# A tuned attention + low-rank FFN kernel: one more matrix product made "joint" over two pairs, its result added by GpSimd, and the memory copy centred after its transpose

## Chip, cores and metric

One core of a Trainium2 chip. The metric is the time on the device, in microseconds (us), of one launch of the whole program; lower is better. The kernel before is at 1116.14 us (median of three runs, 1115.12 to 1116.19).

## What is computed

```python
# x (8, 1024, 1024); ctx (8, 64, 1024); mask (8, 64); all float32
# attention to a small memory, per batch
scores = layernorm(x) @ ctx^T / sqrt(1024), masked to -1e30
x = x + softmax(scores) @ ctx            # zero where no row of the memory is valid
# feed-forward: a dense product and two of eight low-rank experts
h = layernorm(x)
base = h @ W^T                           # 1024 x 1024
w = top-2 of softmax(h @ router^T), normed to sum 1     # 8 experts
x = x + base + 2 * sum_e w_e * (h @ A_e^T) @ B_e^T      # rank 16
```

## The kernel before

**Tiles and pairs.** x has 64 tiles of 128 rows. Two tiles make a pair (32 pairs), four pairs are one batch and share one memory. Pairs 0 and 1 are done in `first()`, the others two at a time in 15 calls of `quad(u)` (u = 2, 4, ..., 30). A quad works on the FFN of pairs u and v = u+1, and beside it on the attention of the pairs that follow: n = u+2, m = u+3, f = u+4. In every other quad (u = 4, 8, ..., 24) f begins a new batch, so that a new memory is set up (`new_mem`).

**Order.** `manual_schedule` keeps the order in which the program text issues instructions. Each engine's queue works in that order and waits at its head. The order is thus written by hand: between products, or in `hooks` that a product calls after one of its blocks of matmuls, stand the small steps of the other pairs. An operation that waits holds up all that stands behind it on its engine.

**The dense product.** Each pair holds the transposed h in two tiles, hA (first half of the 1024 inputs) and hB (second half). With the two tiles as rows, base is a 2 x 2 block product, done in Strassen's form with 7 products in place of 8: GpSimd makes sums of the h blocks (`block_sums`, L566; s1 to s4), the sums of the weights t1 to t4 are made once. Products 1 to 7 of 512 columns are added to x by VectorE where they belong; "product 8" is the low-rank part alone (`lora`, L638). PE writes them into banks of PSUM, of which there are six for this.

**Joint products.** Products 7, 3, 5, 2, 4 of pairs u and v are taken together (`joint`, L720): u above v is a 2 x 2 product again, in halves of 256, and goes by the same form a second time: seven blocks of four matmuls of 256 columns, in place of two products of eight matmuls of 512 columns. The sums of the operands are made by GpSimd too (`joint_sums`, L701), the sums of the weights once (`quarter_sums`, L621). In a joint, `to_x` (L741) adds each part to x from PSUM; products 5 and 7 belong to two places of x (`BOTH`, L686), so each part is added twice.

Product 1 and product 6 are not joint. They run one after the other into one bank "ch" of each pair (`product`, L654): product 1 is added to x at (0,0); then product 6 is accumulated on top, and the bank is added at (0,1) and (1,0) (`chain_add`, L679); then product 8, added at (1,1). (The indices are tile of rows, half of columns.)

**Steps beside them.** `att_turn` (L367) transposes the raw x of a pair for the scores, on VectorE; `att_scores` (L371) is sct on PE and its copy scts on ScalarE; `att_sc` (L389) transposes the scores back on PE; `att_exp` and `att_divide` (L394, L411) are the softmax; `att_turn_p` (L418) transposes it, `att_readout` (L424) multiplies by the memory, `att_add` adds four banks to x. `f_sums`, `f_squares`, `f_std`, `f_rows` (L238 to L276) normalise on ScalarE and send h to DRAM; it comes back in blocks of 32 and `rt_turn_tile` (L502) transposes it. `rt_low_rank_tile` (L518) is the low-rank and router product, `rt_top` (L529) the top-2 weights on VectorE, `rt_turn_low_rank` (L558; trw on PE) turns the weighted result for `lora`.

**The memory.** `load_mem` (L111) loads a batch's ctx twice, for rows 0 to 63 and 64 to 127. A second form, centred (its mean taken off, so that the scores need no mean of x) and transposed, is made over four steps: `mem_stats` (mean), `send_mem` (L320, centred on ScalarE, to DRAM), `fetch_mem` (L332, back in blocks of 32), `turn_mem` (L338, transposed on VectorE). `void_mem` scales the uncentred one by the batch's validity.

Of the kernel before, what the change touches and what calls it, by code (L numbers as in the profile page):

```python
# [24 lines left out]
def kernel(  # L25
# [85 lines left out]
    def load_mem(b: int, halves=(0, 1)):  # L111
        if b not in mems:
            mems[b] = memp.tile([2 * M, D], F32, tag="mem", name=f"mem_{b}")
        for h in halves:
            nc.sync.dma_start(out=mems[b][h * M : (h + 1) * M, :], in_=mem[b])
# [147 lines left out]

    def f_rows(u: int, fetch: bool = True):

        nm, std, of_f = fts.pop(u)
        rstd, nmr = of_f[:, 4], of_f[:, 5]
        nc.vector.reciprocal(rstd, std)
        tt(nmr, nm, rstd, ALU.mult)  # L269
        for r in range(2):  # L270
            h = ring.tile([P, D], F32, tag="ring", name=f"h_{u}_{r}")
            hss.setdefault(u, []).append(h)
            nc.scalar.activation(  # L273
                h, xts[u][r], AF.Identity, bias=nmr[:, r, :], scale=rstd[:, r, :]
            )
        norm_send(u, fetch)  # L276
# [43 lines left out]
    def send_mem(b: int, by_vector: bool = False):  # L320

        if by_vector:
            mc = centre_mem(b, False)
        else:
            mv = mcs[b, "mv"]
            nc.scalar.mul(mv[:M, 1:2], mv[:M, 0:1], -1.0)
            mc = ring.tile([P, D], F32, tag="ring", name=f"memc_{b}_False")
            nc.scalar.activation(mc[:M], mems[b][:M], AF.Identity, bias=mv[:M, 1:2])
        mcs[b] = dram.tile([M, D], F32, tag="md", name=f"md_{b}", bufs=2)
        nc.sync.dma_start(out=mcs[b], in_=mc[:M])  # L330

    def fetch_mem(b: int):  # L332
        msr = ring.tile([P, D], F32, tag="ring", name=f"ms_{b}")
        ms = msr[:, : M // NB * QD].rearrange("p (t c) -> p t c", c=QD)
        load_blocked(ms, mcs[b])
        mcs[b, "ms"] = ms

    def turn_mem(b: int):  # L338
        mt = memp.tile([P, KD, M], F32, tag="memT", name=f"memT_{b}_True", bufs=1)
        transpose_blocked(mt, mcs[b, "ms"])  # L340
        mem_ts[b, True] = mt

# [150 lines left out]
    def h_tiles(u: int):  # L493
        has[u] = turned.tile([P, 2, KH, P], F32, tag="hA", name=f"hA_{u}")
        hbs[u] = turned.tile([P, 2, KH, P], F32, tag="hB", name=f"hB_{u}", bufs=3)

    def rt_turn_pe(u: int, r: int):
        if r == 0:
            h_tiles(u)
        transpose_pe((has[u][:, r], hbs[u][:, r]), hss[u][r], f"h{u}_{r}")  # L500

    def rt_turn_tile(u: int, r: int):  # L502
        if r == 0:
            h_tiles(u)
        half = KH * NB
        for t, c in ((has[u], 0), (hbs[u], half)):
            transpose_blocked(t[:, r], hss[u][r][:, :, c : c + half])
# [10 lines left out]
    def rt_low_rank_tile(u: int, r: int):  # L518
# [3 lines left out]
        for k in range(KD):  # L522
            h = (has[u] if k < KH else hbs[u])[:, r, k % KH, :]
# [42 lines left out]
    def block_sums(outs, a11, a12, a21, a22):  # L566

        s1, s2, s3, s4 = outs

        by = nc.gpsimd.tensor_tensor  # L570

        def one():
            by(s1, a21, a22, ALU.add)  # L573
            by(s2, s1, a11, ALU.subtract)

        def two():
            by(s4, a12, s2, ALU.subtract)  # L577
            by(s3, a11, a21, ALU.subtract)

        return one, two  # L580


    places = ["qa", "qb", "qc", "qd"]

    def in_place(i: int, name: str):
        return sums.tile([P, 2, HK, P], F32, tag=places[i], name=name)

    def rt_sums_steps(u: int, to=(0, 1)):

        sms[u] = sums.tile([P, 2, KH, P], F32, tag="s14", name=f"s14_{u}", bufs=2)  # L590
        s2, s3 = [
            in_place(i, f"s{j}_{u}").rearrange("p h k i -> p (h k) i")
            for i, j in zip(to, (2, 3))
        ]
        outs = sss[u] = sms[u][:, 0], s2, s3, sms[u][:, 1]
        ha, hb = has[u], hbs[u]
        return block_sums(outs, ha[:, 0], hb[:, 0], ha[:, 1], hb[:, 1])
# [3 lines left out]
    def rt_sums(u: int, to=(0, 1)):  # L601
        for do in rt_sums_steps(u, to):
            do()
# [17 lines left out]
    def quarter_sums(name: str, w):  # L621
# [5 lines left out]
        by(q3, b22, b12, ALU.subtract)  # L627
        by(q2, q3, b11, ALU.add)
        by(b12, b12, b11, ALU.subtract)
        by(q4, b21, q2, ALU.subtract)  # L630
        quarters[name] = b11, b21, b22, b12, q2, q3, q4

# [21 lines left out]
    def product(u: int, i: int, between=None, after: int = 0):  # L654
# [8 lines left out]
        elif i == 6:  # L663
            block(chain, sss[u][1], t2, False, between, after)
        elif i == 7:
            block(chain, sss[u][2], t3, False, between, after)
# [12 lines left out]
    def chain_add(u: int):  # L679

        for to in ((0, 1), (1, 0)):
            add(u, pps[u][1], *to)

# [4 lines left out]
    def joint_plain(i: int, p: int, between=None, after: int = 0):  # L688
# [4 lines left out]
            2: (hbs[p][:, 0], w21), 3: (sms[p][:, 1], w22), 4: (hbs[p][:, 1], t4)  # L693
# [4 lines left out]

    jss = {}

    def joint_sums(i: int, u: int):  # L701

        if i == 7:
            s12 = in_place(0, f"s12_j7_{u}")
            s43 = in_place(2, f"s43_j7_{u}")
            outs = jss[7] = s12[:, 0], s12[:, 1], s43[:, 1], s43[:, 0]
            up, lo = [sss[p][2] for p in (u, u + 1)]
            return block_sums(outs, up[:, :HK], up[:, HK:], lo[:, :HK], lo[:, HK:])
        outs = [
            in_place(k, f"s{j}_j{i}_{u}") for k, j in zip((3, 1, 2, 0), (1, 2, 3, 4))  # L710
        ]
        of_pair = sms if i == 5 else hbs
        up, lo = of_pair[u], of_pair[u + 1]
        for r, j in ((0, 5), (1, 3)) if i == 5 else ((0, 2), (1, 4)):
            jss[j] = [o[:, r] for o in outs]
        return block_sums(
            outs, up[:, :, :HK], up[:, :, HK:], lo[:, :, :HK], lo[:, :, HK:]
        )

    def joint(i: int, u: int, hooks, final: bool = False):  # L720
# [4 lines left out]

        v = u + 1
        r, c = L2.get(i, (None, None))
        a, d = [
            {
                2: lambda: hbs[p][:, 0], 3: lambda: sms[p][:, 1], 4: lambda: hbs[p][:, 1],  # L730
                5: lambda: sms[p][:, 0], 7: lambda: sss[p][2],
            }[i]()
            for p in (u, v)
        ]
        s1, s2, s3, s4 = jss.pop(i)
        name = {2: "w21", 3: "w22", 4: "t4", 5: "t1", 7: "t3"}[i]
# [4 lines left out]
        def to_x(p, src, first: int, n: int):  # L741
            for row, col in BOTH.get(i, ((r, c),)):
# [79 lines left out]
    def first():  # L822
# [47 lines left out]
        def plain(r: int, c: int, k: int, between=None):  # L870

            if k == 0:
                banks[r, c] = bank_of(f"plain_{r}_{c}")
            block(
                banks[r, c], (has, hbs)[k][0][:, r], blk[k + 1, c + 1], k == 0, between
# [17 lines left out]
        load_mem(1)  # L893
# [39 lines left out]
        rt_sums(1, (2, 3))  # L933
# [6 lines left out]
        weight_sums((t1, w12, w11, ALU.subtract))  # L940
# [19 lines left out]
        send_mem(1, True)  # L960
        fetch_mem(1)
# [3 lines left out]
        att_readout(3)  # L965
        x_stats(4)
# [5 lines left out]
        void_mem(1)  # L972
# [3 lines left out]
        quarter_sums("t1", t1)  # L976
        product(1, 7)
        quarter_sums("t3", t3)
        product_add(1, 7)
        turn_mem(1)  # L980
# [4 lines left out]
        quarter_sums("w22", w22)  # L985
        product_add(1, 8)
        rt_turn(2)
# [7 lines left out]
        quarter_sums("w21", w21)  # L995
        att_scores(4)

        def last():
            end()
            store(1, 1)  # L1000
            att_rstd(4)
# [6 lines left out]
    def quad(u: int):  # L1008
# [8 lines left out]
        if more and u > 2:  # L1017
            att_turn(m)
            x_sums(m)
        pending.pop()()  # L1020
        product_add(u, 1)
        if u == 2:
            att_divide(n)
        rt_low_rank_tile(u, 0)
        rt_low_rank_tile(u, 1)
        product(u, 6, (lambda: att_turn_p(n)) if u == 2 else None, 1)
        if u == 2:
            att_turn(m)
        if more:
            rt_top(u)  # L1030
            rt_turn(v)
        else:
            rt_turn_tile(v, 0)
            rt_top(u)
            rt_turn_tile(v, 1)
        if more and u > 2:
            x_squares(m)
            x_root(m)
        if new_mem:
            fetch_mem(b)  # L1040
        chain_add(u)
# [3 lines left out]
        if more:  # L1045
            att_readout(n)
            att_scores(m)
            rt_turn_low_rank(u)
            att_add(n)

        low_u = {1: lambda: rt_turn_low_rank(u)}
        if more:
            low_u = {0: lambda: att_sc(m)}
        low_u[2] = lambda: product(u, 8)
        one, two = rt_sums_steps(v, (2, 3))
        one()
        two()
        product(v, 1, low_u)
        if more:
            att_rstd(m)  # L1060
            att_exp(m)
        product_add(u, 8)
        product_add(v, 1)
        one, two = joint_sums(7, u)
        one()
# [3 lines left out]
        if new_mem:  # L1069
            mask_bias(b)  # L1070
            turn_mem(b)
        rt_low_rank_tile(v, 0)
        rt_low_rank_tile(v, 1)
        product(v, 6, (lambda: att_turn_p(m)) if more else None, 1)
        two()
# [5 lines left out]
        chain_add(v)  # L1081
        if more:
            f_std(n)
            f_rows(n)
            att_readout(m)
        if far:
            att_scores(f)
        if more:
            rt_turn_low_rank(v)
            att_add(m)  # L1090
        def low_v():
# [3 lines left out]
        if more:  # L1095
            hooks = {4: [low_v]}
        else:
            hooks = {1: [lambda: rt_turn_low_rank(v)], 3: [low_v]}
        if new_mem:
            void_mem(b)  # L1100
        if (f + 2) % PPB == 0 and f + 2 < NP:
            load_mem((f + 2) // PPB)
            load_mask((f + 2) // PPB)
        if far:
            x_stats(f)
            hooks[3] = [lambda: att_sc(f)]
        end_7 = joint(7, u, hooks)
        one, two = joint_sums(5, u)
        one()
        two()  # L1110

        hooks = {1: [end_7]}
# [3 lines left out]
        if more:  # L1116
            f_sums(m)
# [104 lines left out]
```

## Time and profile before

| | |
|---|---|
| time, median of three runs | 1116.14 us (1115.12 to 1116.19) |
| the profiled execution: time / span | 1115.52 / 1113.7 us |
| granted TensorE clock | 1.00 |
| one quad, from product 1 of u to the next | 67.64 us |
| busy in a quad (443.22 to 510.86): PE, PEld | 67.56, 50.29 us |
| DVE, ACT, POOL | 47.78, 38.17, 23.09 us |

The span is what the profiler recorded of one execution. PE is TensorE's matmuls, PEld its weight loads, DVE is VectorE, ACT ScalarE, POOL GpSimd, SP the queue that issues the DMAs. "L647 ch<-t,s" names the line of the code and the tiles: the output ch from operands t and s. A number behind x counts instructions. In brackets stands the idle time ahead of an instruction and who ended it. A row's duration of a matmul group includes the time in which the last one drains; the difference of two starts tells what a group costs in the queue.

### The profile page before, as it was taken

How to read it: one execution, taken by the hardware profiler on the slowest of the kernel's cores; microseconds unless marked ns; L12 is line 12 of the kernel's file. 1: busy time of each engine (PE TensorE's matmuls, PEld its weight loads, DVE VectorE, ACT ScalarE, POOL GpSimd, SP SyncE). 2: the span in 40 equal slices, each digit the busy share in tenths (PEclk: the TensorE clock that was granted, in tenths of full speed). 3: DMA queues.
4: the chain of work that ended last, by engine and by line, in shares of the span. 5: the costliest groups of instructions: out<-in, count | busy, mean ns of one | idle time of the engine just before them, and what ended most of it. 6: DMA issues, size and time to landing. Idle time of an engine off the chain costs nothing.

```text
span 1113.7 us, 16669 instructions
## 1 busy us (share of the span) xinstructions
PE 1104.8 (99%) x5670; PEld 805.6 (72%) x5670; DVE 771.4 (69%) x2009; ACT 589.2 (53%) x1083; POOL 383.7 (34%) x344
## 2 busy tenths in 40 slices
PE   8999999999999999999999999999999999999998
PEld 6555686776867778687786867768677786877867
DVE  6685777757777676776767767686776767766564
ACT  4577455827458373673827548274583736635010
POOL 0048353234333243233333332343332432333341
PEclk9999999999999999999999999999999999999999
DMA  9956366273653646446373553745446463442401
GB/s 228 228 186 202 116 179 208 76 246 121 182 171 118 210 146 179 144 154 213 107 224 125 160 191 96 246 139 165 150 137 208 149 188 115 154 149 77 151 1 76
DMA packets 105477, 175.80 MB, mean 158 GB/s; under 512 B 13040, under 2 KB 77552, under 8 KB 105392
## 3 DMA queue, kind: packets, MB, share of 16 engines
q1 hardware_dynamic: 105392, 174.73, 50.5%
q8 instruction: 45, 0.74, 0.3%
q14 instruction: 40, 0.33, 0.1%
HBM read 107.84 MB, written 66.85 MB: 157 GB/s over the span
## 4 chain that ended last, share of the span: by engine, by line
PE 98%; DMA 1%; SPq 0%; issue 0%; ACT 0%; DVE 0%; DVEq 0%; ACTq 0%
PE jl L647 24%; PE ch L647 19%; PE ju L647 18%; PE pa L524 11%; PE ro L431 6%; PE sct L377 5%; PE ju L639 3%; PE jl L639 3%; PE plain L647 3%; PE ch L639 2%; PE trw L562 1%; PE j L647 1%; DMA w<-in_w_t_dram 1%; PE b L647 0%; PE plain L639 0%; PE ptp L420 0%
## 5 line engine op out<-in xcount | busy, mean ns | idle before, releaser
L744 DVE TENSOR_TENSOR xt<-jl,xt 128x256 f32<-128x256 f32 (+1 forms) x421 | 191.9, 486 | 130.2 <-PE jl L647 111.7
L744 DVE TENSOR_TENSOR xt<-ju,xt 128x256 f32<-128x256 f32 (+1 forms) x210 | 110.8, 552 | 61.7 <-PE ju L647 60.8
L573 POOL TENSOR_TENSOR s<-hA,hB 128x512 f32<-128x512 f32 x31 | 39.6, 1278 | 306.7 <-DVE hB L89 251.1
L195 ACT ACTIVATE junk<-xt 128x1024 uint8<-128x1024 f32 x60 | 63.3, 1056 | 127.6 <-DMA xt<-in_x_dram 127.1
L647 PE MATMUL ch<-t,s 128*128 128x512 f32 x256 | 116.9, 592 | 0.0
L647 PE MATMUL ch<-w,hA 128*128 128x512 f32 x248 | 115.9, 593 | 0.0
L636 DVE TENSOR_TENSOR xt<-ch,xt 128x512 f32<-128x512 f32 x124 | 82.1, 681 | 20.4 <-PE ch L639 13.1
L647 PE MATMUL jl<-t,s_j 128*128 128x256 f32 x360 | 93.4, 382 | 1.1
L647 PE MATMUL ju<-w,s_j 128*128 128x256 f32 x360 | 94.0, 383 | 0.0
L273 ACT ACTIVATE h<-xt,of_f 128x1024 f32<-128x1024 f32 x60 | 71.3, 1234 | 21.3 <-DVE of_f L269 20.7
L647 PEld LDWEIGHTS jl<-t,s_j 128*128 128x128 f32 x360 | 65.9, 190 | 22.2 <-issue 12.7
L636 DVE TENSOR_TENSOR xt<-ro,xt 128x512 f32<-128x512 f32 x128 | 79.6, 679 | 3.4 <-PE ro L431 3.4
L647 PEld LDWEIGHTS ju<-w,s_j 128*128 128x128 f32 x360 | 64.2, 190 | 16.6 <-DVE xt L744 5.8
L647 PEld LDWEIGHTS ch<-t,s 128*128 128x128 f32 x256 | 45.0, 190 | 42.9 <-issue 42.9
L647 PEld LDWEIGHTS ch<-w,hA 128*128 128x128 f32 x248 | 44.7, 190 | 43.0 <-issue 42.0
L89 DVE STREAM_TRANSPOSE xT<-xs 128x1024 f32<-128x1024 f32 x60 | 72.5, 1228 | 2.7 <-DMA md<-memc_False 1.8
L524 PEld LDWEIGHTS pa<-art_sb,hA 128*128 128x128 f32 x512 | 66.3, 190 | 9.0 <-issue 4.7
L577 POOL TENSOR_TENSOR s_j<-s,s_j 128x256 f32<-128x256 f32 (+1 forms) x30 | 30.1, 1002 | 117.8 <-PE ch L647 96.4
L524 PE MATMUL pa<-art_sb,hA 128*128 128x136 f32 x512 | 69.9, 279 | 0.0
L524 PE MATMUL pa<-art_sb,hB 128*128 128x136 f32 x512 | 69.7, 279 | 0.0
L204 ACT ACTIVATE junk<-xt,of_x 128x1024 uint8<-128x1024 f32 x60 | 68.7, 1145 | 1.5
L253 ACT ACTIVATE junk<-xt,of_f 128x1024 uint8<-128x1024 f32 x60 | 68.5, 1142 | 1.1
(179 smaller groups left out, 2206.4 us busy)
## 6 DMA issues: line engine op xcount, KB each, us to landing
xt<-in_x_dram SPq DMA_DIRECT2D x64, 512.0 KB, 4.6
out_dram<-xt SPq DMA_DIRECT2D x62, 512.0 KB, 3.5
xs<-in_x_dram SPq DMA_DIRECT2D x240, 128.0 KB, 3.6
hd<-h SPq DMA_DIRECT2D x60, 512.0 KB, 2.7
hs<-hd SPq DMA_DIRECT2D x240, 128.0 KB, 3.1
mem<-in_ctx_dram SPq DMA_DIRECT2D x16, 256.0 KB, 4.6
w<-in_w_t_dram SPq DMA_DIRECT2D x16, 256.0 KB, 10.3
md<-memc_False SPq DMA_DIRECT2D x7, 256.0 KB, 3.1
```

The lines of the kernel that those rows point to most:

```text
L89: nc.vector.transpose(dst.rearrange("p k (t i) -> p t k i", i=NB), src.rearrange("p t (k i) -> p t k i", i=NB),)
L195: nc.scalar.activation(nowhere, xts[u][r], AF.Identity, accum_out=sm[:, r, :])
L204: nc.scalar.activation(nowhere, xts[u][r], AF.Square, bias=nm[:, r, :], accum_out=ss[:, r, :],)
L253: nc.scalar.activation(nowhere, xts[u][r], AF.Square, bias=nm[:, r, :], accum_out=ss[:, r, :])
L273: nc.scalar.activation(h, xts[u][r], AF.Identity, bias=nmr[:, r, :], scale=rstd[:, r, :])
L377: mm(sct[r * M : (r + 1) * M, :], mt[:, k, :], x_ts[u][r][:, k, :], start=(k == 0), stop=(k == KD - 1),)
L431: mm(ro, pts[u][rows, :], m[rows, ts(c, HB)], start=True, stop=True)
L524: mm(pa[:, r, :], h, art_sb[:, k, :], start=(k == 0), stop=(k == KD - 1))
L636: tt(xc, bank, xc, ALU.add)
L639: mm(bank, axwts[u][:, r, :], lb_sb[:, c0 : c0 + n], start=alone, stop=True, skip_group_check=True)
L647: mm(bank, a[:, k, :], w[:, k, :], start=(start and k == 0), stop=(k == n - 1), skip_group_check=True)
L744: tt(xc, src, xc, ALU.add)
```

## The change

**Product 6 becomes joint**, as the first: the joints now go 6, 2, 7, 3, 5, 4. Its result isn't added to x by VectorE part by part, but put into a place of its own, t: the first half of hA, whose content is no longer needed by then (`t_of`). One 256-column part is copied by ScalarE, the other three by VectorE, and two of 512 columns are then added to t by VectorE. Then GpSimd adds t to x at three places for each of the two pairs (`six_add`, six adds of 128 x 512). Product 1 is added at (0,0), (0,1) and (1,0) by VectorE (`one_add`).

**Sums in place.** The third sum of a pair (`rt_sum_3`) overwrites hA's second half, that of a joint the half of the lower operand; joint sums are made for one product at a time. hB becomes a tile for each tile of rows.

**One memory copy.** The centred memory isn't sent to DRAM. `load_ms` loads ctx in blocks of 32 directly, `turn_mem` transposes it on VectorE and sums it over its eight chunks, `centre_turned` multiplies by ones of 1/1024 on PE (the mean of each row, in all partitions), and VectorE subtracts. The uncentred memory has one buffer, loaded after the last readout of the old one.

**Moved steps.** `att_turn_p` stands between the two low-rank tiles; `rt_turn_low_rank(u)` right after `att_scores(m)`; `rt_turn_low_rank(v)` in joint 6; `att_turn(m+2)` in joint 4 of the quad before; `f_rows(n)` in two steps in joint 6. In `first()`, GpSimd makes t1 and the sums of t2's quarters.

```diff
+    def load_ms(b: int):
+        msr = ring.tile([P, D], F32, tag="ring", name=f"ms_{b}")
+        n = M // NB * QD
+        ms = msr[:, :n].rearrange("p (t c) -> p t c", c=QD)
+        load_blocked(ms, mem[b])
+        ones = msr[:, n : n + P]
+        nc.gpsimd.memset(ones, 1.0 / D)
+        mcs[b] = ms, ones, msr[:, n + P : n + P + M]
     def turn_mem(b: int):
         mt = memp.tile([P, KD, M], F32, tag="memT", name=f"memT_{b}_True", bufs=1)
-        transpose_blocked(mt, mcs[b, "ms"])
+        ms, ones, of_k = mcs[b]
+        transpose_blocked(mt, ms)
+        nc.vector.tensor_reduce(of_k, mt.rearrange("p k m -> p m k"), AX.X, ALU.add)
         mem_ts[b, True] = mt
+    def centre_turned(b: int):
+        ms, ones, of_k = mcs.pop(b)
+        mt = mem_ts[b, True]
+        means = bank_of(f"means_{b}")[:, :M]
+        mm(means, ones, of_k, start=True, stop=True)
+        tt(mt, mt, means.unsqueeze(1).to_broadcast([P, KD, M]), ALU.subtract)
...
+    def one_add(u: int):
+        for to in ((0, 0), (0, 1), (1, 0)):
             add(u, pps[u][1], *to)
+    def t_of(u: int):
+        return has[u][:, 0].rearrange("p k i -> p (k i)")
+    def six_add(u: int):
+        for r, c in ((1, 0), (1, 1), (0, 1)):
+            xc = xts[u][r][:, ts(c, HB)]
+            nc.gpsimd.tensor_tensor(xc, xc, t_of(u), ALU.add)
...
         def to_x(p, src, first: int, n: int):
+            if i == 6:
+                t = t_of(p)[:, first : first + n]
+                if n == HH and p == u and first == 0:
+                    nc.scalar.copy(t, src)
+                elif n == HH:
+                    nc.vector.tensor_copy(t, src)
+                else:
+                    tt(t, src, t, ALU.add)
+                return
...
         product(u, 1, (lambda: att_sc(n)) if u == 2 else None, 1)
         if more and u > 2:
-            att_turn(m)
             x_sums(m)
+        if new_mem:
+            mask_bias(b)
         pending.pop()()
-        product_add(u, 1)
...
+        one_add(u)
         rt_low_rank_tile(u, 0)
...
         rt_low_rank_tile(u, 1)
-        product(u, 6, (lambda: att_turn_p(n)) if u == 2 else None, 1)
...
+        rt_turn_tile(v, 0)
+        rt_top(u)
+        rt_turn_tile(v, 1)
+        rt_sum_3(u)
+        rt_sums(v)
...
         if new_mem:
-            fetch_mem(b)
-        chain_add(u)
+            load_ms(b)
...
             att_readout(n)
             att_scores(m)
-            rt_turn_low_rank(u)
+            if u > 2:
+                rt_turn_low_rank(u)
+                x_root(m)
             att_add(n)
...
         product(v, 1, low_u)
...
             f_sums(n)
             att_divide(m)
         if new_mem:
-            mask_bias(b)
             turn_mem(b)
+        one_add(v)
         rt_low_rank_tile(v, 0)
+        if more:
+            att_turn_p(m)
+        if new_mem:
+            centre_turned(b)
         rt_low_rank_tile(v, 1)
-        product(v, 6, (lambda: att_turn_p(m)) if more else None, 1)
-        two()
+        joint_sums(6, u)
+        rt_sum_3(v)
         if far:
             att_turn(f)
         rt_top(v)
...
             att_readout(m)
         if far:
             att_scores(f)
+        if new_mem:
+            load_mem(b)
         if more:
-            rt_turn_low_rank(v)
             att_add(m)
+        hooks = {5: [lambda: rt_turn_low_rank(v)]}
...
+        end_6 = joint(6, u, hooks)
+        joint_sums(2, u)
+        def six():
+            end_6()
+            low_v()
+            for p in (u, v):
+                six_add(p)
+        hooks = {1: [six]}
...
-        end_7 = joint(7, u, hooks)
+        end_2 = joint(2, u, hooks)
+        joint_sums(7, u)
...
+        if m + 2 < NP:
+            hooks[5] = [lambda: att_turn(m + 2)]
         end_4 = joint(4, u, hooks, not more)
```

## The prediction

> **What bounds the kernel now.** I read the page's engine line and its chain of waits first, then PE's waits, then three equal stretches, then the timeline of one stretch.
>
> ```profile
> PE 1104.8 (99%) x5670; PEld 805.6 (72%) x5670; DVE 771.4 (69%) x2009; ACT 589.2 (53%) x1083; POOL 383.7 (34%) x344
> PE 98%; DMA 1%; SPq 0%; issue 0%; ACT 0%; DVE 0%; DVEq 0%; ACTq 0%
> ```
>
> PE is busy for 99% of the span, and the chain that ended last is PE for 98% of it. Any time is gained or lost on PE's queue: fewer matmuls, or a wait that PE doesn't have today. It has almost none: PE's longest waits are 1.6 us at the start and this one.
>
> ```profile
> PE ptp L420 <- DVE s L415: 1.0, 1, 1.0
> ```
>
> The stretches run from one product 1 of an even pair to the next, so each is one quad.
>
> ```profile
> 375.58:443.22 67.64, 67.56 (x353) 50.29 (x352) 48.02 (x125) 38.47 (x70) 23.11 (x21) 1.00 0.53 161
> 443.22:510.86 67.64, 67.56 (x353) 50.29 (x352) 47.78 (x126) 38.17 (x69) 23.09 (x21) 1.00 0.52 167
> 510.86:578.50 67.64, 67.56 (x353) 50.29 (x352) 48.01 (x125) 38.48 (x70) 23.10 (x21) 1.00 0.52 161
> ```
>
> The columns are PE, PEld, DVE, ACT, POOL, granted clock. The period is 67.64 us whether or not a new memory is set up (the middle one does it), at full clock. DVE has 20 us free, POOL 44 us. Fifteen such quads are the program; pairs 0 and 1 come before.
>
> **The matmuls.** One full product is 8 matmuls of 512 columns, and a joint one has seven blocks of 4 matmuls of 256 columns in place of two products.
>
> ```profile
> 450.80 3.60 PE L647 MATMUL ch<-t,s 128*128 128x512 f32 x8
> 454.33 1.99 PE L431 MATMUL ro<-mem,pt 64*128 64x512 f32 x8
> 456.25 1.97 PE L377 MATMUL sct<-xT,memT_True 128*64 128x128 f32 x32
> 458.15 0.44 PE L562 MATMUL trw<-ident,axl 128*128 128x128 f32 x2
> ```
>
> The first row is product 6. From its start to the next is 3.53 us, of which 0.09 is a gap that stands before ro anyway: 3.44. A block of a joint starts every 0.865 us (422.58, 423.44, 424.31 in the same timeline). Product 6 costs 2 x 3.44 = 6.88 us per quad now and 7 x 0.865 = 6.06 after: -0.82 us per quad, 15 quads, **-12.4 us**. Joints 5 and 7 lose 0.25 us each to waiting for two 256-column adds; joint 6 has one copy there, so I count none (to +0.25 a quad, 3.7 in all).
>
> **POOL.** Per quad it had 23.1 us. It gets: 8 adds of 512 columns for the sums of a pair (1.27 each), 24 of 256 for six joints (0.73), 6 of 512 that add t to x (1.27): 10.2 + 17.5 + 7.6 = 35.3 us, 52% of 67. Walked in its order, the sums of each joint are ready before it; the tightest is joint 7, whose s1 stands behind the six adds, ready 39.6 us after the quad's start and wanted at 41.5. Cost 0; if every such add were half slower, joint 7 would wait about 1.9 us a quad.
>
> **The cover that goes.** With product 6 go twice 3.44 us in which PE was busy while DVE made the top-2 weights, the softmax and the transposes. I put zero at the start of product(u,1), use start-to-start durations of the 443 us stretch, and walk PE: product 3.44, one lora 0.43, two low-rank tiles 1.85 each: 7.57; gap 0.09, readout 1.92, scores 1.90: trw is asked for at 11.48; trw 0.27, product(v,1) with sc in it 3.55, product 8 0.86: 16.16; low-rank tile 18.01; ptp 0.11; second tile, gap and readout: scores of f (sct) asked for at 22.0. DVE beside it:
>
> ```profile
> 451.42 0.24 DVE L535 MAX8 top<-axl 128x8 f32<-128x8 f32 x2 [2.84 <-ACT axl L527]
> ...
> 454.36 0.70 DVE L89 STREAM_TRANSPOSE hA<-hs 128x512 f32<-128x512 f32 x1
> ...
> 457.95 2.47 DVE L636 TENSOR_TENSOR xt<-ro,xt 128x512 f32<-128x512 f32 x4
> ...
> 465.06 0.71 DVE L89 STREAM_TRANSPOSE memT_True<-ms 128x512 f32<-128x512 f32 x1 [0.35 <-issue]
> 465.69 2.33 DVE L89 STREAM_TRANSPOSE xT<-xs 128x1024 f32<-128x1024 f32 x2
> ```
>
> The top-2 chain starts 0.62 us after the last low-rank tile and takes 2.94: it ends at 11.13, with 0.15 to 0.2 us for the semaphore trw is just in time. Then one tile's transposes 1.23, four readout adds 2.39, the score operations of the softmax 1.05, exp on ACT 0.8, reciprocal and division 0.4, three adds of product 1 at 0.597, two transposes of 1.125: end at 21.1 to 21.2. sct is asked for at 22.0: 0.8 us spare. The score transpose sc has 0.15 to 0.25 spare behind ACT's copy, ptp 1.0. So a **regular quad** waits nothing, or some tenths where a slack of 0.2 is missed. Below it can't go; above, all of trw, sc and sct together by their latencies gives 0.5. I take 0.2 for eight quads: +1.6 (0 to 4).
>
> **The new memory** (quads 4, 8, ..., 24, six of them). The old copy went out to DRAM and back, its centring on ACT, and its transpose lay under product 6. Now DVE has, in the same stretch ahead of sct, the transpose (0.63 by the rows above, 465.06 to 465.69), the sum over 8 chunks and the subtraction. Neither sum nor subtraction of 512 elements is in the trace: the reduce rows go from 0.22 (64 elements) to 0.286 (128), whose slope gives 0.69; the 512-column add from PSUM gives 0.60. Bounds from the same rows: 0.29 (no growth) to 1.27 (twice as slow as an add). The sum of means is one more matmul on PE, 0.11. DVE ends at 21.2 + 0.63 + 0.69 + 0.60 = 23.1, sct would be at 22.1: PE waits about 1.1, with the matmul +1.2 per quad. The ones that POOL writes for it push the sums of joint 6 over the division, which reads SBUF twice, as these rows do:
>
> ```profile
> 56.88 0.69 DVE L613 TENSOR_TENSOR t<-t,w 128x512 f32<-128x512 f32 x1
> 57.49 1.76 DVE L613 TENSOR_TENSOR t<-w,w 128x512 f32<-128x512 f32 x1
> 59.28 1.64 DVE L613 TENSOR_TENSOR t<-t,w 128x512 f32<-128x512 f32 x1
> ```
>
> and POOL at the same time:
>
> ```profile
> 57.25 1.45 POOL L573 TENSOR_TENSOR s<-hA,hB 128x512 f32<-128x512 f32 x1 [55.68 <-ACT hB L353]
> 58.78 1.60 POOL L574 TENSOR_TENSOR s<-s,hA 128x512 f32<-128x512 f32 x1
> ```
>
> DVE's add of two SBUF tiles goes from 0.69 to 1.76 and 1.64 beside POOL's 1.45 and 1.60, in step with them. Adds from PSUM don't: four readout adds take 2.47 beside POOL at 458 and 2.48 at 473 with POOL idle. The division can so wait up to one POOL add of 256, 0.73: 1.2 to 1.8 per quad; I take 1.55: **+9.3** for six (0.7 each, 4.2, with a reduce of 0.29 and no collision; 2.4 each, 14.4, with 1.27).
>
> At two places a rule stands beside these rows. The Trainium skill, "SBUF — State Buffer", section "SBUF: two separate sides", says that VectorE's operations with two SBUF inputs and a GpSimd operation that reads SBUF hold one port pair in turn, each for its whole instruction. The rows agree in direction (0.95 to 1.07 us lost per add); by that rule every collision costs what is left of one POOL instruction, 1.8 for all six memories, and the sum would be 1.5 us higher. The Trainium skill, "GPSIMD Engine Reference", section "4.1 Engine selection", speaks against six_add: elementwise adds belong on VectorE, GpSimd being about half as fast with two inputs (here 1.27 against 0.60). By it DVE takes six adds, 3.6 us of its 20 free ones; PE's sum is the same either way as long as both have room.
>
> **Quad u=2** keeps its scores, division and transposes in the first half, now without product 6: DVE's chain meets trw about 0.55 late, ptp of the other pair about 1.5, sct 0.1: +2.2 (1 to 3.5). **The last quad** turns its low-rank part right after product(v,1) and its product 8 waits for ACT's copy: +0.7 (0.3 to 1.5). **Pairs 0 and 1**: one means matmul, +0.1; t1 moves from DVE to POOL, and POOL is busy with quarter sums until about 117 us, each ready before its first joint (t1 by 73, wanted at 82): 0, and if t1 came late, +1 to 4.
>
> **Moved at no cost.** The joints' order, split hB tiles, third sums in place: the same matmuls. SP loses a 256 KB store per memory and gets no other bytes; the memory comes after the readout of m and is wanted only in the next quad, over 20 us later, while such loads land in 4.6 us. f_rows(n) stands now behind joint 6's first copy on ACT; rows are wanted half a quad later. If that cover were gone, hB transposes late by x would move rt_sums by x, with 1.7 us spare.
>
> **Sum**: -12.4 + 9.3 + 1.6 + 2.2 + 0.7 + 0.1 = +1.5 us on 1115.52 of the profiled execution, which is 0.6 under the median of 1116.14; a last us for the 0.25 in joint 6 that I set aside a quarter likely. So 1118 on the median.
>
> **Rivals.**
> - *Faster: the cover holds.* DVE and ACT have 20 and 29 us free per quad, and the spare of 0.8 before sct is real; the reduce costs 0.3, no collision. Then -12.4 + 4.2 + 1 + 0.3 + 0.1 = -6.8: 1109; with no wait at all 1104. Against it: the memory's operations are in a row with sct. Chance 0.29, around 1104 to 1113.
> - *Slower: trw and sct in every quad.* The one mechanism is DVE's chain from the top-2 weights to the transposes of f; it decides from 0.2 us at trw and 0.8 at sct. If POOL's sums, now 35 us a quad, stretch its SBUF operations by one add (0.7) at the top-2 chain and one at the division, PE waits 0.5 + 0.3 in each of 14 quads, and 0.5 more in the six: 1118 - 1.6 + 14 x 0.8 + 3 = 1131; half of it, 1124. For it: POOL's rows above. Against: POOL waits for the transposes during most of the top-2 chain. Chance 0.24, from 1122 up.
> - *POOL late*: joint 7 waits behind the six adds, 1.9 a quad, 28 in all: 1146. Chance 0.03.
> - *Gain and waits cancel*, the forecast, 1113 to 1122: chance 0.44.
>
> **Numbers.** 0.2% (2.2 us) is about what a measurement of this kernel can tell from no change. Of the forecast's 0.44, 0.24 lies within it and 0.20 above; with the rivals: faster 0.29, same 0.24, slower 0.47. The range 1107 to 1127 leaves out the lowest of the first rival and the upper end of the second.
>
> **Signs.** Right: regular quads last 66.8 to 67.2, those with a memory 68 to 69, PE's waits named sct and means; POOL near 52%; blocks of joint 6 at 0.865. Wrong: waits at trw or sc of half a us in every quad, blocks of joint 7 waiting for POOL, or six quads with no wait at sct.

## The result, and the profile after

The changed kernel takes 1119.88 us (median of five runs, 1119.62 to 1122.07), the one before 1115.70 in the same comparison: the ratio is 1.0042 (95% interval 1.0027 to 1.0057). That is slower by 0.42%, 4.2 us. The forecast was 1118 in a range of 1107 to 1127.

The page of the profiled execution (span 1117.9 us, 1113.7 before) has these two lines in the places of the two that the prediction began with:

```profile
PE 1099.6 (98%) x5864; PEld 844.7 (76%) x5864; DVE 822.1 (74%) x2072; ACT 554.0 (50%) x1060; POOL 567.8 (51%) x629
PE 88%; DVE 7%; POOL 2%; issue 1%; DMA 1%; ACT 1%; SPq 0%; DVEq 0%; ACTq 0%; POOLq 0%
```

PE has 5.2 us less work, and yet the span is 4.2 us longer: 9.4 us in which PE isn't busy are new. In the chain of waits PE fell from 98% to 88%, and DVE stands in it with 7%. That points at VectorE, but it is a share of the chain and not of the waiting (7% of the span would be 78 us). PE's own list of waits names the instructions:

```profile
PE means L366 <- DVE ms L358: 3.7, 6, 0.6
PE ptp L446 <- DVE s L441: 1.9, 2, 1.0
PE trw L593 <- DVE axl L587: 1.8, 2, 1.5
```

The numbers behind the colon are the us in total, how many waits, and the longest. One ptp of 1.0 stood there before; the means, trw and the other ptp are new. Two neighbouring quads, the first without and the second with a new memory, in the columns PE, PEld, DVE, ACT, POOL and clock:

```profile
241.52:308.57 67.05, 66.83 (x365) 52.76 (x364) 49.56 (x128) 35.05 (x67) 34.66 (x38) 1.00 0.51 158
308.57:377.12 68.55, 67.71 (x368) 53.19 (x367) 53.03 (x134) 35.98 (x68) 34.82 (x39) 1.00 0.53 166
```

Both were 67.64 before. The quad without a memory is 0.60 faster, the one with a memory 0.91 slower. From the starts of product 1 of u in both timelines the whole difference adds up:

| part of the span | change, us |
|---|---|
| up to quad 2 | -0.2 |
| quad 2 (67.54 to 68.09) | +0.6 |
| six quads with a new memory (4 to 24), +0.91 each | +5.4 |
| six quads without (6 to 26), -0.60 each | -3.6 |
| quad 28 (65.86 to 65.16) | -0.7 |
| quad 30, to the end of the span (63.5 to 66.2) | +2.7 |
| sum | +4.2 |

### The profile page after: what moved, and what is told of

It reads as the page before. It is cut to its first block, busy times and chain, and to the rows that moved or that the text cites. A ratio compares the mean times of both kernels' runs of the same rounds, so it can differ in the third digit from the quotient of the medians.

```text
span 1117.9 us, 17572 instructions
## 1 busy us (share of the span) xinstructions
PE 1099.6 (98%) x5864; PEld 844.7 (76%) x5864; DVE 822.1 (74%) x2072; ACT 554.0 (50%) x1060; POOL 567.8 (51%) x629
## 4 chain that ended last, share of the span: by engine, by line
PE 88%; DVE 7%; POOL 2%; issue 1%; DMA 1%; ACT 1%; SPq 0%; DVEq 0%; ACTq 0%; POOLq 0%
PE jl L675 25%; PE ju L675 19%; PE pa L555 9%; PE ch L675 9%; PE sct L403 5%; PE ro L457 5%; PE ju L667 3%; PE jl L667 3%; PE plain L675 3%; PE ch L667 2%; DVE xt L789 2%; POOL xt L719 1%; PE j L675 1%; DVE xt L664 1%; PE trw L593 1%
## 5 line engine op out<-in xcount | busy, mean ns | idle before, releaser
L789 DVE TENSOR_TENSOR xt<-jl,xt 128x256 f32<-128x256 f32 x421 | 191.3, 484 | 116.2 <-PE jl L675 76.8
L789 DVE TENSOR_TENSOR xt<-ju,xt 128x256 f32<-128x256 f32 (+1 forms) x210 | 110.6, 550 | 66.5 <-PE ju L675 64.8
L719 POOL TENSOR_TENSOR xt<-xt,hA 128x512 f32<-128x512 f32 x90 | 111.3, 1270 | 25.9 <-DVE hA L785 25.9
L614 POOL TENSOR_TENSOR hA<-hA 128x512 f32<-128x512 f32 x31 | 39.5, 1273 | 148.2 <-PE pa L555 148.2
L675 PE MATMUL ju<-t,s_j 128*128 128x256 f32 x360 | 93.7, 383 | 2.2
L664 DVE TENSOR_TENSOR xt<-ch,xt 128x512 f32<-128x512 f32 x124 | 79.6, 681 | 14.9 <-PE ch L667 8.7
L675 PEld LDWEIGHTS ju<-t,s_j 128*128 128x128 f32 x360 | 65.0, 190 | 16.7 <-POOL s_j L755 7.3
L675 PE MATMUL jl<-t,s 128*128 128x256 f32 x300 | 76.0, 384 | 0.0
L403 PEld LDWEIGHTS sct<-xT,memT_True 128*64 128x64 f32 x960 | 52.9, 137 | 24.1 <-issue 12.1
```

What stands on the lines that cost most here:

```text
L403: mm(sct[r * M : (r + 1) * M, :], mt[:, k, :], x_ts[u][r][:, k, :], start=(k == 0), stop=(k == KD - 1),)
L664: tt(xc, bank, xc, ALU.add)
L675: mm(bank, a[:, k, :], w[:, k, :], start=(start and k == 0), stop=(k == n - 1), skip_group_check=True)
L719: nc.gpsimd.tensor_tensor(xc, xc, t_of(u), ALU.add)
L789: tt(xc, src, xc, ALU.add)
```

## Where a new memory's time goes

PE in the second of those quads. The bracket names the idle time ahead of an instruction and who ended it:

```profile
326.59 0.27 PE L446 MATMUL ptp<-ident,s 128*128 128x128 f32 x1
327.48 0.41 PE L366 MATMUL means<-ms 128*128 128x64 f32 x2 [0.62 <-DVE ms L358]
...
331.64 2.38 PE L403 MATMUL sct<-xT,memT_True 128*64 128x128 f32 x32
```

DVE in the same stretch:

```profile
324.99 0.65 DVE L441 TENSOR_TENSOR s<-s,of_s 128x128 f32<-128x128 f32 x1
325.56 0.70 DVE L89 STREAM_TRANSPOSE memT_True<-ms 128x512 f32<-128x512 f32 x1
326.29 1.05 DVE L358 TENSOR_REDUCE ms<-memT_True 128x64 f32<-128x512 f32 x1
327.25 1.87 DVE L664 TENSOR_TENSOR xt<-ch,xt 128x512 f32<-128x512 f32 x3
329.05 0.68 DVE L367 TENSOR_TENSOR memT_True<-memT_True,means 128x512 f32<-128x512 f32 x1
329.64 1.24 DVE L89 STREAM_TRANSPOSE xT<-xs 128x1024 f32<-128x1024 f32 x1
```

PE reaches the means 0.78 us before their sum is there. Its matmul (two instructions) and a slower start behind it cost 0.30, and the scores of f then last 2.31 us to the next instruction in place of 1.90, since the transposes of f end only at 332.0: 1.49 in all. The sum over the chunks (L358) takes 1.05; the division (L441) takes 0.65, where it took 0.29 before and takes 0.50 in the neighbouring quad.

## The experiments

The theory after this reading: (1) the joint form gives PE its 0.8 us per quad; (2) VectorE's sum and subtraction for a new memory, in a row with the transposes of f, cost six quads 1.5 each; (3) the last quad loses because GpSimd stretches the top-2 weights that trw waits for. The rival for all three: the denser work of GpSimd slows things everywhere, and the joint form eats its own gain. All ratios are against the kernel before, with the 95% interval.

### Product 6 as two plain products

```diff
-        joint_sums(6, u)
-        end_6 = joint(6, u, hooks)
+        for p in (u, v):
+            bank = bank_of(f"six_{p}")
+            step = 2 if p == u else 5
+            block(bank, sss[p], t2, True, lambda: [do() for do in hooks.get(step, ())], 2 if p == u else 1)
+            nc.vector.tensor_copy(t_of(p), bank)
```

> The changed kernel, with product 6 as two plain products of 8 matmuls of 512 columns in a bank each, copied to t by VectorE; its joint sums and the quarter sums of t2 are gone, all else stays. My theory: the joint form saves TensorE 6.88 - 6.06 = 0.82 us a quad, less 0.1 to 0.2 that the profile after shows between its first two blocks and the next joint: this kernel is 15 x (0.6 to 0.8) = 9 to 12 us slower than the changed one, about 1129 to 1132 us, and the six quads with a new memory keep their extra 1.5 us. Rival: the joint form costs as much beside it as it saves (its sums on GpSimd collide with VectorE, its copies hold up blocks); then this kernel is within 3 us of the changed one, 1117 to 1123.

1126.75 us, ratio 1.0108 (1.0093 to 1.0124): 6.9 more than the changed kernel, between the two expectations. The quads tell why. Those without a memory go from 67.05 to 67.89, +0.84, the full gain of the joint form. Those with one go from 68.55 to 69.03 only (+0.48), and the last becomes 1.7 us faster. So the joint form pays 0.36 of its gain back in each of the six, and in the last quad it costs 1.7 more than it saves. In the six, GpSimd has no joint sums beside the division, and it takes 0.29 again in place of 0.65. In the last quad the top-2 weights of v take 4.3 us in place of 5.8, trw is asked for later, and PE doesn't wait there. The theory holds for the size per quad, and the rival has a part of the sum.

### No centring of new memories

```diff
         transpose_blocked(mt, ms)
-        nc.vector.tensor_reduce(of_k, mt.rearrange("p k m -> p m k"), AX.X, ALU.add)
...
-        mm(means, ones, of_k, start=True, stop=True)
-        tt(mt, mt, means.unsqueeze(1).to_broadcast([P, KD, M]), ALU.subtract)
```

> The changed kernel without the centring of new memories: no sum over the chunks, no matmul of the means, no subtraction (this part of the computation is left out); load, ones and transpose stay. My theory: VectorE's 0.96 + 0.59 us and the wait for the means are what holds up the scores of f, since the transposes of f then end at 21.8 us of the quad where TensorE asks for them at 22.0: the six quads with a new memory fall from 68.55 to 67.05 to 67.2, in all -8 to -9 us, about 1111 us. Rival: the collision of the softmax division with GpSimd, 0.57 us in place of 0.21, and the memory's transpose do it; then at most 2 us are won, 1118 us or more.

1112.49 us, ratio 0.9972 (0.9963 to 0.9981), 7.4 less than the changed kernel. The six quads are at 67.06, like their neighbours, 8.9 us less in all. (The profiled execution lost 1.9 of it again ahead of quad 2; its granted clock was 0.57 to 0.58 between 8 and 12 us. Three executions with a mean clock of 1.00 took 1111.3.) The quads fell though the transpose, the ones and the collision at the division are still there:

```profile
325.43 0.64 DVE L437 TENSOR_TENSOR s<-s,of_s 128x128 f32<-128x128 f32 x1
325.99 0.70 DVE L89 STREAM_TRANSPOSE memT_True<-ms 128x512 f32<-128x512 f32 x1
326.62 1.84 DVE L660 TENSOR_TENSOR xt<-ch,xt 128x512 f32<-128x512 f32 x3
328.39 2.34 DVE L89 STREAM_TRANSPOSE xT<-xs 128x1024 f32<-128x1024 f32 x2
```

The division takes 0.64 as in the changed kernel, and the transposes of f still end in time. So it is the sum, the matmul and the subtraction, as the theory has it; the 0.36 of the experiment before shows that the longer division costs only where they stand behind it.

### Two more GpSimd adds beside the top-2 weights

```diff
         rt_sum_3(u)
+        if more and u > 2:
+            for _ in range(2):
+                nc.gpsimd.tensor_tensor(sms[u][:, 1], hbs[u][0], sss[u], ALU.subtract)
         rt_sums(v)
```

> The changed kernel with two more GpSimd adds of 128 x 512 in each of 13 quads, ahead of the sums of v, where GpSimd now waits (8.2 to 12.1 us of the quad); they write again what is there. My theory: VectorE's top-2 weights of u stand beside them and stretch from 2.55 us to 3.5 to 5.8, as in the last quad beside GpSimd; TensorE's trw, with 0.7 us to spare, waits 0.3 to 2.4 us a quad: +4 to +30 us, 1124 to 1150, and the wait bears the name trw. Rival: the small operations don't collide, or 0.7 us are enough: 1119 to 1121.

1138.16 us, ratio 1.0204 (1.0190 to 1.0218): +18.3 for 32 us more of GpSimd's work, at a time when it is otherwise idle. PE's waits, and in one quad VectorE's rows beside GpSimd's two adds (251.55 to 254.16):

```profile
PE trw L593 <- DVE axl L587: 13.2, 15, 1.5
PE means L366 <- DVE ms L358: 7.9, 6, 1.3
```

```profile
251.61 0.24 DVE L566 MAX8 top<-axl 128x8 f32<-128x8 f32 x2 [0.43 <-ACT axl L558]
251.89 0.94 DVE L569 TENSOR_TENSOR of_top<-top 128x2 f32<-128x2 f32 x1
...
253.15 1.04 DVE L574 CAST of_top<-idx 128x4 f32<-128x4 uint32 x1
254.22 0.26 DVE L578 TENSOR_TENSOR we<-iota_e,of_top 128x16 f32<-128x16 f32 x2
```

Two operations of two and four columns, 0.16 and 0.17 us alone, take 0.94 and 1.04, each to about the end of a GpSimd add; behind the second one all are as short as ever. The quad without a memory becomes 0.95 longer; the one with a memory 1.65, as PE now waits 1.3 at the means too. The theory holds, and the mechanism of the prediction's slower rival is real. The changed kernel escapes it in its regular quads, since GpSimd waits for the transposes while the top-2 weights of u are made.

### The six adds on VectorE

```diff
-                six_add(p)
...
+                tt(xc, xc, t_of(p), ALU.add)
...
+            4: [lambda: adds((u, 1, 0), (u, 1, 1))],
+            6: [lambda: adds((u, 0, 1), (v, 1, 0))],
+            7: [lambda: adds((v, 1, 1), (v, 0, 1))],
```

> The changed kernel with the six adds of t to x on VectorE, two each at three places of joint 2, in place of GpSimd; GpSimd has 7.6 us a quad less. My theory: no term of TensorE's sum is touched; VectorE has room, but an add behind which a part of the joint waits can cost some tenths: 1119 to 1123, and the last quad as slow as in the changed kernel. Rival, by the rule that elementwise adds belong on VectorE: its adds are half as long and GpSimd's sums come sooner, so the time falls, to 1117 or less.

1148.24 us, ratio 1.0291 (1.0277 to 1.0306). Neither expectation holds; it is 28 us slower, 1.85 in each quad from 4 to 26. VectorE's row, then GpSimd's of the changed kernel:

```profile
L1166 DVE TENSOR_TENSOR xt<-xt,hA 128x512 f32<-128x512 f32 x90 | 80.0, 928 | 0.0
```

```profile
L719 POOL TENSOR_TENSOR xt<-xt,hA 128x512 f32<-128x512 f32 x90 | 111.3, 1270 | 25.9 <-DVE hA L785 25.9
```

An add takes 0.93 us on average, not 0.60, for it reads SBUF twice and stands in part beside GpSimd's sums for the joints. In one quad, VectorE's adds and GpSimd's sums:

```profile
420.52 1.28 DVE L1166 TENSOR_TENSOR xt<-xt,hA 128x512 f32<-128x512 f32 x2
422.06 2.36 DVE L1166 TENSOR_TENSOR xt<-xt,hA 128x512 f32<-128x512 f32 x2
```

```profile
422.02 0.72 POOL L756 TENSOR_TENSOR s_j<-s,s_j 128x256 f32<-128x256 f32 x1 [3.17 <-PE ju L675]
422.70 1.17 POOL L757 TENSOR_TENSOR s<-s,s 128x256 f32<-128x256 f32 x1
423.84 1.17 POOL L754 TENSOR_TENSOR s_j<-s 128x256 f32<-128x256 f32 x1
```

Two adds take 1.28 while GpSimd is idle and 2.36 beside its sums. PE's new waits are mostly for parts of the joints that stand behind the adds in VectorE's queue (L789; 8.4 us before jl and 6.0 before ju in the trace). How the 28 us divide between the stretched adds and the queue wasn't tested. Other places in the joints were not tried either, so this says that VectorE's place was bad, not that every one is.

### The memory centred ahead of its turning

```diff
         transpose_blocked(mt, ms)
-        nc.vector.tensor_reduce(of_k, mt.rearrange("p k m -> p m k"), AX.X, ALU.add)
...
+        for t in range(2):
+            nc.scalar.activation(nowhere[:, :QD], ms[:, t, :], AF.Identity, accum_out=of_t[:, t : t + 1])
...
-        mm(means, ones, of_k, start=True, stop=True)
-        tt(mt, mt, means.unsqueeze(1).to_broadcast([P, KD, M]), ALU.subtract)
+        mm(means, ones, of_t[:, 0:2], start=True, stop=True)
+        nc.scalar.mul(of_t[:, 2:4], means, -1.0 / D)
+        for t in range(2):
+            nc.scalar.activation(ms[:, t, :], ms[:, t, :], AF.Identity, bias=of_t[:, 2 + t : 3 + t])
```

Here "ones" has 1 where two partitions hold the same rows, so the matmul adds the four column blocks.

> The changed kernel with the new memory centred ahead of its turning: loaded at the quad's start, summed by ScalarE in its block layout, one matmul of the means between the low-rank tiles of u, subtracted by ScalarE; VectorE only transposes it where it did. My theory (the sum and the subtraction on VectorE, in a row with the transposes of f, cost the six quads 1.5 us each): they fall from 68.55 to 67.1 to 67.5, with 0.1 to 0.2 for the matmul; in all -6 to -9 us, 1111 to 1114, faster than the kernel before. Rival: any step for the memory ahead of the scores of f costs about the same wherever it runs (the transpose alone takes the slack); then the quads stay above 68.2 and the time above 1118.

1130.88 us, ratio 1.0151 (1.0124 to 1.0178): missed. The quads did fall (67.28 to 68.40), but quad 2 began at 119.6 us in place of 104.9. ScalarE's sums waited at the head of its queue for a load that hadn't come, and PE waited for what stood behind them. PE's longest wait, and ScalarE's first sum:

```profile
PE ro L471 <- ACT pt L462: 7.6, 1, 7.6
```

```profile
85.95 0.42 ACT L361 ACTIVATE junk<-ms 128x256 uint8<-128x256 f32 x1 [8.95 <-DMA ms<-in_ctx_dram]
```

The same with the last quad rearranged (next section) fared alike:

> Both of these together. My theory: the two lie in different quads and add up: -8 to -11 us against the changed kernel, 1109 to 1112. Rival: no more than the better of the two, 1112 or more.

1128.80 us, ratio 1.0116 (1.0100 to 1.0131), with quad 2 beginning at 120.9. Mended, the sums standing behind the load and the matmul behind both low-rank tiles:

```diff
+        sum_ms(1)
         f_sums(3)
...
         rt_low_rank_tile(u, 1)
+        if new_mem:
+            centre_ms(b)
```

> As the memory centred ahead of its turning, mended in two places that its profile named: before the first quad ScalarE's sums stood in its queue ahead of a load that waited for a buffer and held up all behind it, 14.7 us; they now stand after it has landed. In the quads the matmul of the means waited up to 0.9 us for that load; it now stands after both low-rank tiles of u. My theory: start at 105 us as in the changed kernel, six quads at 67.2 to 67.5: 1111 to 1114, faster than the kernel before by 0.2 to 0.4%. Rival: the early load itself costs, in the quads or ahead of them: above 1116.

1116.33 us, ratio 1.0001 (0.9992 to 1.0009): 3.6 less than the changed kernel, but not the 1111 to 1114 expected. The six quads are at 67.17, 1.37 less than in the changed kernel, as the theory has it: ScalarE can bear this work, VectorE can't in that stretch. But quad 2 rose from 68.09 to 70.92: pair 3's rows now waited behind the centring (tested below). And the last quad of the profiled execution took 1.8 longer, most of it at a lower granted clock (last section).

### The last quad

```diff
-                if n == HH and p == u and first == 0:
+                if n == HH and (v + 1 == NP or (p == u and first == 0)):
                     nc.scalar.copy(t, src)
...
-        hooks = {5: [lambda: rt_turn_low_rank(v)]}
+        hooks = {5: [lambda: rt_turn_low_rank(v)]} if more else {}
...
         end_6 = joint(6, u, hooks)
+        if not more:
+            joint_sums(7, u)
+            end_7 = joint(7, u, {1: [end_6], 5: [lambda: rt_turn_low_rank(v)]})
         joint_sums(2, u)
```

> The changed kernel with its last quad rearranged: joint 7 ahead of joint 2, the turning of v's low-rank part in joint 7 in place of joint 6, the four copies of joint 6 by ScalarE. My theory: the last quad's 3.5 us too many are mostly TensorE's wait at trw in joint 6 (1.49 + 0.34 us by the profile, 2.2 with what follows) for top-2 weights that GpSimd stretches from 2.6 to 5.8 us; now nothing in joint 6 waits for them: -1.5 to -2.5 us, about 1118 us, all of it after the last product 1 of u. Rival: the wait moves to joint 7 or 2, where GpSimd's sums are as dense: 0 to -0.7 us.

1117.24 us, ratio 1.0014 (1.0005 to 1.0023), 2.6 less, as the theory has it: the last quad falls from 66.17 to 63.67, the others stay. What it took away, in the changed kernel's PE, VectorE and GpSimd rows:

```profile
1074.43 0.30 PE L593 MATMUL trw<-ident,axl 128*128 128x128 f32 x1 [1.49 <-DVE axl L587]
```

```profile
1070.03 0.49 DVE L574 CAST of_top<-idx 128x4 f32<-128x4 uint32 x1
1070.56 0.75 DVE L578 TENSOR_TENSOR we<-iota_e,of_top 128x16 f32<-128x16 f32 x2
1071.22 1.23 DVE L579 TENSOR_SCALAR of_top<-of_top 128x2 f32<-128x2 f32 x1
1072.49 0.17 DVE L580 RECIPROCAL of_top<-of_top 128x2 f32<-128x2 f32 x1
```

```profile
1071.14 1.29 POOL L614 TENSOR_TENSOR hA<-hA 128x512 f32<-128x512 f32 x1
```

The tensor_scalar of two columns starts 0.08 after GpSimd's add and ends with it; the reciprocal behind it is as fast as ever. The top-2 weights of v take 5.8 us here, 2.6 in the kernel before. In the rearranged quad they still take 5.9, but trw comes later and waits for nothing:

```profile
1079.63 0.38 PE L593 MATMUL trw<-ident,axl 128*128 128x128 f32 x2
```

In the changed kernel the two waits, with the slower start behind them, had cost 2.4 us, about the whole of the gain. The order and the place of the copies were changed together, so what the copies are worth isn't shown.

### A version that beats both

> The same with the rearranged last quad, which by itself took 2.6 us off. My theory: they add up, 1108 to 1111. Rival: no more than one of them, 1112 or more.

1112.11 us, ratio 0.9975 (0.9961 to 0.9988): above the 1108 to 1111 expected, at the rival's bound. By the quads the two do add up (the six at 67.17, the last at 63.64); what is missing is quad 2, still at 70.92.

And with memory 1 centred ahead of the sums of pair 3:

```diff
         sum_ms(1)
+        product(1, 7, lambda: centre_ms(1), 6)
         f_sums(3)
         f_squares(3)
         f_std(3)
-        product(1, 7)
+        turn_mem(1)
...
-        centre_ms(1)
-        turn_mem(1)
```

> As the memory centred ahead of its turning with the rearranged last quad, but before the first quad ScalarE centres memory 1 ahead of the sums of pair 3, not behind them: there its profile showed the rows of pair 3 sent 4.7 us later, and TensorE waiting 1.7 and 1.4 us in quad 2 (70.92 us in place of 68.07). My theory: quad 2 goes back to 68.0 to 68.3: -2.6 to -2.9 us, 1109 to 1110. Rival: ScalarE's 1.9 us ahead of pair 3 are late anyway and quad 2 stays above 69.5: 1111 or more.

1110.28 us (1109.40 to 1113.68), ratio 0.9959 (0.9945 to 0.9972): 5.4 us faster than the kernel before, 9.6 faster than the changed one. Quad 2 fell to 68.45, 0.15 above the expected range; quad 26 took 0.57 longer, with a wait of 0.50 in a joint, so that the time lies 0.3 above the 1109 to 1110 expected. The same two quads:

```profile
241.96:309.02 67.06, 66.84 (x365) 52.76 (x364) 49.58 (x128) 34.97 (x68) 34.80 (x39) 1.00 0.52 158
309.02:376.19 67.17, 66.94 (x367) 52.97 (x366) 50.79 (x132) 38.04 (x76) 35.91 (x41) 1.00 0.54 168
```

The quad with a memory is 0.11 longer than its neighbour. Against that quad of the changed kernel DVE has 2.2 us less and ACT 2.1 more; PE's waits no longer name means, and the scores of f take 1.90 again. Undoing the memory part alone, with the old round trip through DRAM, wasn't tried.

## Why the prediction was right, and where not

- **PE's gain**, -0.82 a quad: right. The plain products cost 0.84 more in the quads where nothing else differs. The 0.22 that regular quads lose was in the sum as 0.2, but I had put it at trw and sc, and in eight quads. It lies in the joints, and comes in the quads with a memory too (2.8 us in all, not 1.6): joint 6's first two blocks take 1.83 in place of 1.73, and joints 7 and 5 wait 0.69 together, not 0.56.
- **The cover in regular quads**: right, and without the tenths that I had set aside. trw was asked for at 11.48 and sct at 21.99 after the quad's start, as walked, and neither waited.
- **The new memory**, 1.2 to 1.8, taken as 1.55: measured 1.50. The parts were off and made up for each other: the sum over chunks 0.96 start to start (0.69 from the slope), the division 0.57 (up to 0.94 allowed), the transpose 0.73 (0.63). The matmul of the means is two instructions, 0.24, not 0.11. The wait moved as well: I had put about 1.1 at sct, but 0.78 stands at the means and 0.41 at sct.
- **Quad 2**: +2.2 predicted over the gain, 1.4 measured; one wait of 0.9 at ptp, not three.
- **The last quad** is the step that failed: "+0.7 (0.3 to 1.5)" was 3.5. I named product 8's wait (0.46, as seen) and put nothing at trw of v in joint 6, as if the top-2 weights of v kept their old length; there it was 2.4. In that quad no readout and no scores stand between the low-rank tiles and trw, and GpSimd runs without a pause. The collision that I priced as a rival for every quad met the top-2 weights here alone. At the division it came in every quad (0.39 to 0.67 in place of 0.29), but cost PE something only in the six with a memory (0.36, by the two plain products).
- **The sum**: +1.5 was 4.3 on the profiled execution. The last quad's miss alone is 2.8, so that the rest of the sum looks exact; that is partly luck. Quad 2 (-0.8), the memory (-0.3) and the part up to quad 2 (-0.3) came out lower, the joints higher (+1.2). And with the last us that I added for joint 6 my terms give 1118.6, not 1118.
- **The rivals**: "the cover holds" fails by the six quads with a memory; with their sum gone (no centring) the time is 1112.5, nearer its 1109. "POOL late" didn't come: PE waits for no sum of joint 7.
- **The six adds**: the page's advice to put them on VectorE was priced at nothing for PE; it costs 28 us in the place tried, where parts of the joints waited behind the adds and GpSimd's sums stretched them.

## What to carry over

Walk the end of a program as a schedule of its own: the steps that hid a wait are missing there, while the engines that caused it are at their busiest. When work is moved to GpSimd, list which small VectorE operations will stand beside it, and price each at the GpSimd instruction it can meet, not at its own 0.2 us. Extra work on the engine whose chain ends just ahead of the critical one belongs on another engine, but every step that waits for a load must stand behind what can go first in that queue.

## What the runs showed of the hardware

- Beside GpSimd adds, VectorE's add of two SBUF tiles, its cast and its tensor_scalar were stretched to as much as the GpSimd instruction's length (0.16 to 1.23 us at most), while find-index (0.15), reciprocal (0.17), max (two in 0.24), transposes (0.70) and adds from PSUM (four in 2.45 to 2.48) kept theirs. GpSimd's own adds were stretched too, from 0.73 to 1.17, beside VectorE's six adds. The Trainium skill, "SBUF — State Buffer", section "Who interferes with whom", names, beside operations with two SBUF inputs, copy, cast and tensor_scalar as able to contend with GpSimd when their operands meet certain conditions. The cast and the tensor_scalar of these rows agree; for a copy between SBUF tiles no row is shown here. I had used only the part on two inputs.
- After PE's wait at trw in the last quad, the granted clock fell in some executions. In the profiled one of the mended memory kernel (stretches of 2 us, columns as above, the clock third from the right):

```profile
1071.00:1073.00 2.00, 2.00 (x8) 1.66 (x7) 0.00 (x0) 0.00 (x0) 0.00 (x0) 0.63 0.04 8
1073.00:1075.00 2.00, 2.00 (x6) 1.56 (x6) 1.55 (x3) 0.00 (x0) 0.46 (x1) 0.51 0.00 0
1075.00:1077.00 2.00, 2.00 (x9) 1.39 (x8) 0.64 (x2) 0.00 (x0) 2.00 (x2) 1.00 0.00 0
```

  Two blocks took 1.7 us each in place of 0.865, 1.7 us in all; the slow stretch began about 1.3 us after the start of the second trw, ahead of which PE had waited 1.50 and 0.34. The profiled execution with the six adds on VectorE shows the same after the same waits (0.50 between 1102 and 1104 us). But that of the changed kernel has these waits and keeps 1.00, and without centring the clock kept 1.00 there and fell between 8 and 12 us. So the wait is not enough by itself, and a mean clock of 0.998 doesn't say where it fell. In 8 of the 12 executions of the mended kernel the mean was 0.998, and those took 1116.1 to 1116.9; the others took 1114.7 to 1116.0. With the last quad rearranged, none of 11 executions of the changed kernel were at 0.998, but one of 8 of the first version with both parts was, and one at 0.997. That the wait causes the fall is therefore likely, not shown. The Trainium skill, "TensorE: Matmul & The Clock Gate", section "Part 1: The HAM clock gate", describes half rate after an idle window of about 3.4 us. The half rate agrees (0.51); the waits here were shorter than that window.
